# Order of the second batch's query pairs, and a fifth kind of pair by seven products

## The chip, the cores and the metric

The kernel runs on one core of a Trainium2 chip. A core has a matrix engine (TensorE, PE in the profile), a vector engine (VectorE, DVE), an activation engine (ScalarE, ACT), a general engine (GpSimd, POOL) and a queue that starts transfers (SyncE, SP). Each works through its own list of instructions in order; semaphores tie the lists together. Matrix products are written to PSUM[...]; everything else lies in SBUF. The metric is the device time of one execution in microseconds, as a median of several.

## The reference

The input x has 2 batches of 2048 rows of 512 numbers. It is normalised twice for an attention with one head of width 512 and a causal mask, and once for a mixture of experts whose output gates the attention's. All of it is computed in float32.

```python
xn = _layernorm(x)
# attention: a second norm, then
q, k, v = x_norm @ qkv[:, :512], x_norm @ qkv[:, 512:1024], x_norm @ qkv[:, 1024:]
scores = where(causal, q @ k.T / sqrt(512), -inf)      # per batch, 2048 x 2048
s = softmax(scores) @ v @ o_proj + xn
# experts: top 2 of 8, hidden width 352
g = silu(sum over the two experts of gate * expert(xn))
out = x + s * g
```

## The kernel before

The program first normalises all rows and makes keys, queries and values, which go to DRAM; then it runs the experts; the last part, from about 572 us on, is the attention, and only this part is touched by the change. The output projection has been folded into the values, so that attention ends with probabilities times values.

The attention works on tiles of 128 query rows. A batch has 16 tiles, 0 to 15, and 4 blocks of 512 keys. Tile t needs the key blocks before its own in full and its own block up to the diagonal, 128(t+1) keys in all. The list `seq` (line 1010) gives the tile of each of the 32 steps: the first batch in steps 0 to 15 from tile 15 down to tile 0, the second batch in steps 16 to 31 as line 1011 says. Two neighbouring tiles, an even one and the next, always follow each other: a pair. The blocks of the second batch are numbered 4 to 7, so K = 4 in the text below is the first of them.

In the loop at line 1756, step s does this for its tile:

- Scores. `chunk_scores` (line 1298) makes the scores of one key block, up to 512 wide, with four matrix products into a PSUM tile `ps`; a mask on the diagonal (line 1308) and a row maximum (line 1291) follow on VectorE. Pairs listed in `SCORED` (line 1267) go another way for their first two key blocks: `fast_scores` (line 1338) makes a 2 by 2 block product of the pair with seven half-size products (`p7`, line 1355) instead of eight, from sums of query parts (`query_sums`, line 1316, tile `sq`, made in the step before) and sums of key parts (`block_sums`, line 1327, tile `tk`, made once a batch). Each product is two calls 512 wide. The results are put together on VectorE (line 1361) in the tile `pT` in SBUF, both tiles of a pair at once in the pair's even step. ScalarE starts that with a copy of the first product (line 1374).
- `end_scores` (line 1389) negates the maximum; `exponentials` (line 1474) has ScalarE make the probabilities, piece by piece (line 1481).
- Turning. Probabilities must be transposed for the product with the values. Wide tiles go by GpSimd (line 1491, splitting the bytes), a transposing DMA (line 1497) and VectorE (`join_p`, line 1511). Tiles 0, 1 and 2 are transposed by TensorE one step later (`turn_p`, line 1504), with a copy by ScalarE (line 1509).
- Values, two steps later. `values` (line 1518) multiplies by one tile of 128 keys at a time, 512 wide, line 1531. Pairs in `FAST` (line 1268: those in `SCORED`, and pair 4 of the list) go by seven half-size chains instead (`values_first`, `values_next`, `values_end`, lines 1600 to 1651), from sums of probabilities (`combine_p`, line 1555) and sums of value parts (`combine_v`, line 1544, tile `vT`).
- Output. `divisor` sums and inverts (line 1653); `attended` scales on ScalarE (line 1692) and adds the residual on VectorE (line 1695); `emit` multiplies by the gate and adds x on GpSimd (lines 1703 and 1704) and stores. `gate` (line 1679) makes the gate of a pair: two scalings on ScalarE (line 1684), two sums on VectorE (line 1685), one Silu (line 1687). `gather_y` (line 1667) has GpSimd fetch the experts' rows.

The order of all this is written out by hand in the loop. Key and value blocks of the second batch are fetched while the first batch runs, by the list `parts_b` (line 1736): block 6 in steps 4 and 6, block 5 in steps 8 and 10, block 4 in steps 12 and 14, block 7 in steps 20 and 22. The table `later` (line 1742) says after which steps' exponentials the sums of key and value parts of the second batch are made, one part at a time. PSUM has two pools here: `ps_a` with five buffers for scores, `ps_b` with three for values; buffers are given in turn, so a product waits until the reader of the tile five places earlier is done.

Of the kernel before, what the change touches and what calls it, by code (L numbers as in the profile page):

```python
# [26 lines left out]
def gated_attention_moe(  # L27
# [33 lines left out]
    BT = 4  # L61
    TB = BT * P
    NB = NT // BT
    NBB = S // TB
# [943 lines left out]

    assert B == 2 and NBB == 4
    seq = [t for t in reversed(range(NBB * BT))]  # L1010
    seq += [NBB * BT + t for t in (8, 9, 0, 1, 6, 7, 2, 3, 4, 5, 10, 11, 12, 13, 14, 15)]
    assert all(seq[s] // 2 == seq[s + 1] // 2 for s in range(0, NT, 2))
    fetch_k = fetch(aks, lambda: kp2, kt_d, "k2", "kT")
    fetch_v = fetch(avs, lambda: vp, v_d, "v2", "v")
# [249 lines left out]
    OUT = 4  # L1264


    SCORED = (0, 1, 2, 3, 13, 14, 15)
    FAST = SCORED + (4,)

    def place(s):  # L1270
# [23 lines left out]
    def direct(s):  # L1294

        return range(2 if s // 2 in SCORED else 0, len(widths[s]))

# [18 lines left out]
    def query_sums(s, engine):  # L1316

        q = qsums[s] = sq.tile([P, 4, ND // 2, P], F32, name=f"sq_{s}", tag="sq")
        (a11, a12), (a21, a22) = (
            [aqs[seq[s] // 2][:, d, ts(seq[s + i] % 2, P)] for d in kds] for i in range(2)  # L1320
        )
        engine.tensor_tensor(q[:, 0], a21, a22, ALU.add)
        engine.tensor_tensor(q[:, 1], q[:, 0], a11, ALU.subtract)
        engine.tensor_tensor(q[:, 2], a11, a21, ALU.subtract)
        engine.tensor_tensor(q[:, 3], a12, q[:, 1], ALU.subtract)
# [341 lines left out]
    def gather_y(s):  # L1667

        rows[s] = [op.tile([P, 2, D], F32, name=f"yg0_{s}", tag="yg0")]
        for i in range(2):  # L1670
            rows[s].append(op.tile([P, D], F32, name=f"yg1_{s + i}", tag="yg1"))
            n = seq[s + i]
            for k, y in enumerate((rows[s][0][:, i, :], rows[s][-1])):
                nc.gpsimd.indirect_dma_start(  # L1674
                    out=y, out_offset=None, in_=y_d,
                    in_offset=bass.IndirectOffsetOnAxis(ap=posi[k][:, n : n + 1], axis=0),
                )
# [57 lines left out]
    K = NBB  # L1735
# [6 lines left out]
    later = {}  # L1742
    for steps, f, b in (
        ((10, 10, 11, 11), combine_v, K + 2), ((12, 12, 13, 13), combine_v, K + 1),
        ((20, 21, 22, 23), block_sums, K), ((24, 25, 26, 27), combine_v, K),
    ):
        for i, step in enumerate(steps):
            later.setdefault(step, []).append((f, b, (i + 1,)))
# [7 lines left out]
    for s in range(NT + OUT + 2):  # L1756
        fast = s // 2 - 1 in FAST
        pair = (s, s + 1) if s // 2 in SCORED else (s,)
        if s < NT and (s % 2 == 0 or len(pair) == 1):
# [30 lines left out]
        if s == NT - 1:  # L1790
            gather_y(NT - 2)
        if s % 2 and s > 3 and s // 2 + 1 in SCORED:
            query_sums(s + 1, nc.vector)
# [143 lines left out]
```

## Time and profile before

| what | us |
|---|---|
| median of 3 runs | 1010.59 |
| lowest and highest of them | 1010.33, 1010.79 |
| the profiled execution in all | 1012.02 |
| its span | 1010.3 |
| start of step 16 on TensorE (second batch) | 781.53 |
| start of the first pair by seven products in the second batch | 870.00 |
| end of TensorE's last product | 1006.48 |

The span runs from the first to the last instruction that the profile shows. All times below are microseconds from its start. A line of the timeline gives start, duration, engine, line of the program, operation, output and inputs without their numbers, and how often it came in a row; in brackets stands the idle time before it and who ended it. In the chain of waits each line is a stretch of the chain of work that ended last, with start, duration, engine, tile and line. A float32 matrix product appears as two records.

From 781.5 to 897.5 us, the steps that the change reorders, TensorE has no gap:

```profile
core 0: us, PE busy (x) PEld busy (x) DVE busy (x) ACT busy (x) POOL busy (x), PEclk, DMA share, GB/s
781.50:870.00 88.50, 88.50 (x247) 43.95 (x246) 54.35 (x98) 42.98 (x74) 66.45 (x55) 1.00 0.78 223
870.00:897.50 27.50, 27.50 (x68) 12.57 (x67) 22.58 (x44) 9.89 (x17) 15.15 (x13) 1.00 0.60 147
```

The columns are the stretch, its length, the busy time of each engine with the number of instructions, the clock that TensorE was granted, and the DMA engines' share and rate.

### The profile page before, as it was taken

To read this page: it belongs to the slowest core of one execution; us is meant where nothing else is said; L and a number is where in the kernel's file an instruction comes from. 1 tells how busy PE (TensorE), PEld (TensorE's weight loads), DVE (VectorE), ACT (ScalarE), POOL (GpSimd) and SP (SyncE) were. 2 spreads that over 40 slices of the span, in tenths; PEclk is the share of its full clock that TensorE was granted. 3 is DMA by queue.
4 is the path that set the end of the run, shared out by engine and by line. 5 is a ranking of instruction groups with operands and counts; after the bars stand their busy time and mean duration, and the time that the engine had idled before them with its cause. 6 is when DMAs were issued, how large, how long until landed. Compare 5 with 4: busy or idle time off the path is not lost. (4 is left out here: it accounts for less than half of the span.)

```text
span 1010.3 us, 13408 instructions
## 1 busy us (share of the span) xinstructions
PE 1001.5 (99%) x3924; PEld 665.7 (66%) x3924; DVE 719.6 (71%) x1396; ACT 402.7 (40%) x804; POOL 481.6 (48%) x475
## 2 busy tenths in 40 slices
PE   9999999999999999999999999999999999999998
PEld 5887888874577677667653448677675544447577
DVE  6997755896877777776744669678576457878667
ACT  3354455322444544444455122232345544442241
POOL 4474465003744444443432256164557776764272
PEclk9999999999999999999999999999999999999999
DMA  8799987979999999999999576373677768753361
GB/s 291 234 240 319 319 237 268 331 254 230 182 247 213 205 219 218 210 211 214 213 213 254 162 191 149 90 189 110 186 199 233 224 202 241 204 146 86 95 164 42
DMA packets 295495, 207.96 MB, mean 206 GB/s; under 512 B 230648, under 2 KB 243704, under 8 KB 294400
## 3 DMA queue, kind: packets, MB, share of 16 engines
q1 hardware_dynamic: 280128, 155.17, 62.1%
q0 software_dynamic: 10400, 34.63, 12.6%
q10 hardware_dynamic: 4896, 17.30, 4.6%
q8 instruction: 34, 0.56, 0.2%
q14 instruction: 37, 0.30, 0.1%
HBM read 92.35 MB, written 60.03 MB: 151 GB/s over the span
## 5 line engine op out<-in xcount | busy, mean ns | idle before, releaser
L1191 PE MATMUL py<-arena,ht 128*128 (+3 forms) x396 | 176.7, 593 | 0.0
L1303 PE MATMUL ps<-k,q 128*128 128x512 f32 (+3 forms) x416 | 143.0, 495 | 0.3 <-PEq L1451 0.3
L1491 POOL COPY pu<-pT 128x1024 uint16<-128x1024 uint16 (+2 forms) x74 | 81.8, 1137 | 119.1 <-ACT pT L1481 59.2
L1162 POOL COPY hu<-h 128x704 uint16<-128x704 uint16 x66 | 61.8, 954 | 155.8 <-issue 121.7
L1191 PEld LDWEIGHTS py<-arena,ht 128*128 128x128 f32 (+3 forms) x396 | 71.8, 185 | 80.6 <-issue 76.4
L1303 PEld LDWEIGHTS ps<-k,q 128*128 128x128 f32 x416 | 74.7, 190 | 67.1 <-issue 56.3
L966 POOL DMA_INDIRECT xs<-zu_d,toki x66 | 77.7, 1177 | 70.6 <-DVE toki L793 55.9
L1177 ACT ACTIVATE ht<-ht,b1sel 128x128 f32<-128x128 f32 (+3 forms) x216 | 67.9, 380 | 88.4 <-DVE ht L1171 88.4
L1141 DVE TENSOR_TENSOR h<-p,h 128x176 f32<-128x176 f32 x182 | 55.4, 336 | 59.6 <-PE p L1134 56.1
L1674 POOL DMA_INDIRECT yg<-y_d,posi x64 | 67.3, 1052 | 36.9 <-DVE yg L1685 22.0
L1531 PE MATMUL po<-v,pT 128*128 128x512 f32 x152 | 67.9, 592 | 0.0
L347 POOL COPY zu<-z 128x1024 uint16<-128x1024 uint16 x32 | 39.4, 1230 | 57.7 <-DVE z L332 57.7
L1481 ACT ACTIVATE pT<-pT,nm 128x1024 f32<-128x1024 f32 x14 | 16.1, 1148 | 110.3 <-DVE nm L1391 72.0
L1513 DVE COPY pT<-puT 128x1024 uint16<-128x1024 uint16 (+2 forms) x74 | 53.4, 750 | 7.4 <-DMA puT<-pu 7.2
L1199 ACT COPY y<-py 128x512 f32<-128x512 f32 x55 | 32.1, 584 | 62.1 <-PE py L1191 48.2
L1481 ACT ACTIVATE pT<-ps,nm 128x512 f32<-128x512 f32 (+3 forms) x52 | 30.0, 580 | 60.4 <-DVE nm L1391 36.7
L1361 DVE TENSOR_TENSOR pT<-p,pT 128x512 f32<-128x512 f32 x49 | 32.9, 687 | 25.8 <-PE p L1355 22.1
L1531 PEld LDWEIGHTS po<-v,pT 128*128 128x128 f32 x152 | 28.6, 190 | 31.9 <-issue 30.1
L1042 DVE COPY xT<-xhT 128x1024 uint16<-128x1024 uint16 x66 | 44.7, 703 | 6.4 <-DMA xhT<-xs 6.3
L1703 POOL TENSOR_TENSOR o<-o,yg 128x512 f32<-128x512 f32 x30 | 41.4, 1380 | 14.3 <-DVE o L1695 14.2
L1695 DVE SCALAR_TENSOR_TENSOR o<-xo,xscale,o 128x512 f32<-128x512 f32 x30 | 25.9, 871 | 30.1 <-ACT o L1692 30.1
L1704 POOL TENSOR_TENSOR o<-o,xo 128x512 f32<-128x512 f32 x30 | 43.2, 1439 | 2.4
(342 smaller groups left out, 2146.9 us busy)
## 6 DMA issues: line engine op xcount, KB each, us to landing
y_d<-y SPq DMA_DIRECT2D x66, 256.0 KB, 4.3
zu_d<-zu SPq DMA_DIRECT2D x32, 264.0 KB, 3.2
kt_d<-kT ACTq DMA_DIRECT2D x8, 1024.0 KB, 8.2
q<-qt_d SPq DMA_DIRECT2D x32, 256.0 KB, 5.0
k<-kt_d SPq DMA_DIRECT2D x32, 256.0 KB, 4.2
v<-v_d SPq DMA_DIRECT2D x32, 256.0 KB, 5.7
xo<-in_x_dram SPq DMA_DIRECT2D x32, 256.0 KB, 4.0
x<-in_x_dram SPq DMA_DIRECT2D x30, 256.0 KB, 6.5
```

What stands on the lines that cost most here:

```text
L966: nc.gpsimd.indirect_dma_start(out=xs, out_offset=None, in_=zu_d, in_offset=bass.IndirectOffsetOnAxis(ap=toki[:, order[i] : order[i] + 1], ...
L1042: nc.vector.tensor_copy(xT.bitcast(U16).rearrange("p c (t h) -> p c t h", h=2), xhs.pop(i).rearrange("p (h c) t -> p c t h", h=2),)
L1141: nc.vector.tensor_tensor(out, x, y, ALU.add)
L1162: nc.gpsimd.tensor_copy(hu[:, :, :H], h.bitcast(U16).rearrange("p (d h) -> p h d", h=2))
L1177: nc.scalar.activation(ht[:hn, c, at], ht[:hn, c, at], AF.Silu, bias=b1sel[:hn, c, j : j + 1])
L1191: nc.tensor.matmul(py[at, :], lhsT=ht[:k, c, at], rhs=rhs[n], start=(c == 0), stop=(c == NH - 1),)
L1303: nc.tensor.matmul(ps[:, :w], lhsT=aqs[seq[s] // 2][:, c, ts(t % 2, P)], rhs=aks[first + j][:, c, :w], start=(c == 0), stop=(c == ND - 1),)
L1481: nc.scalar.activation(turned[s][:, at:end], src, AF.Exp, bias=nm, accum_out=rs[:, j : j + 1])
L1491: nc.gpsimd.tensor_copy(pu[:, : 2 * w].rearrange("p (h d) -> p h d", h=2), turned[s][:, k : k + w].bitcast(U16).rearrange("p (d h) -> p h ...
L1513: nc.vector.tensor_copy(turned[s][:, k : k + w].bitcast(U16).rearrange("p (i t h) -> p i t h", t=P, h=2), puT[:, : 2 * w // P, :].rearrang ...
L1531: nc.tensor.matmul(dst, lhsT=turned[s][:, ts(k, P)], rhs=avs[first + k // BT][:, k % BT, cols], start=(start and k == k0), stop=(k == k1 - 1),
L1674: nc.gpsimd.indirect_dma_start(out=y, out_offset=None, in_=y_d, in_offset=bass.IndirectOffsetOnAxis(ap=posi[k][:, n : n + 1], axis=0),)
```

## The change

The pairs of the second batch come in another order, pair 8-9 moves from the front to the fifth place (steps 24 and 25) and is listed in `SCORED`, and so in `FAST`; it had been scored and multiplied in full. The value sums of block 4 move from steps 24 to 27 to steps 16 to 19, the key sums from steps 20 to 23 to steps 19 to 22. Pairs 10-11, 12-13 and 14-15 keep their steps, and the fetches keep theirs.

```diff
     seq = [t for t in reversed(range(NBB * BT))]
-    seq += [NBB * BT + t for t in (8, 9, 0, 1, 6, 7, 2, 3, 4, 5, 10, 11, 12, 13, 14, 15)]
+    seq += [NBB * BT + t for t in (6, 7, 4, 5, 0, 1, 2, 3, 8, 9, 10, 11, 12, 13, 14, 15)]
...
-    SCORED = (0, 1, 2, 3, 13, 14, 15)
+    SCORED = (0, 1, 2, 3, 12, 13, 14, 15)
     FAST = SCORED + (4,)
...
-        ((20, 21, 22, 23), block_sums, K), ((24, 25, 26, 27), combine_v, K),
+        ((16, 17, 18, 19), combine_v, K), ((19, 20, 21, 22), block_sums, K),
```

## Prediction

> **What bounds the kernel now.** I read the table of engines first, then the chain of waits in order of time, then VectorE's and ScalarE's timelines from 835 to 920 us, where the change acts.
>
> ```profile
> PE 1001.5 (99%) x3924; PEld 665.7 (66%) x3924; DVE 719.6 (71%) x1396; ACT 402.7 (40%) x804; POOL 481.6 (48%) x475
> ```
>
> TensorE works all the time; the others are partly idle. So time is saved by fewer TensorE instructions, and lost wherever TensorE has to wait. The chain shows both:
>
> ```profile
> 781.53 7.76 PE ps L1303 x24
> 789.29 1.72 PE po L1531 x4
> 791.01 0.11 PE pt L1508
> ...
> 870.00 12.02 PE p L1355 x28
> 882.02 2.58 PE ps L1303 x8
> 884.60 4.29 PE po L1531 x10
> ...
> 897.47 12.02 PE p L1355 x28
> ...
> 913.81 4.32 PE p L1579 x20
> ```
>
> Step 16, the first of the second batch, begins at 781.53, and from there each piece starts where the last one ended: no wait. A matmul call gives two records. A 512-wide call costs 12.02/14 = 0.859 us, a 256-wide one 4.32/10 = 0.432, and 128, 256 and 384 columns of scores (four calls) 0.89, 1.73 and 2.58. With these I can place every piece of a new order.
>
> The other engines are the danger:
>
> ```profile
> 845.64 2.37 DVE L1336 TENSOR_TENSOR tk<-k 128x1024 f32<-128x1024 f32 x1
> 847.93 1.75 DVE L1695 SCALAR_TENSOR_TENSOR o<-xo,xscale,o 128x512 f32<-128x512 f32 x1
> 865.58 1.25 DVE L1322 TENSOR_TENSOR sq<-q 128x256 f32<-128x256 f32 x1
> 866.86 0.50 DVE L1323 TENSOR_TENSOR sq<-sq,q 128x256 f32<-128x256 f32 x1
> 867.29 1.48 DVE L1324 TENSOR_TENSOR sq<-q 128x256 f32<-128x256 f32 x1
> 868.69 1.48 DVE L1325 TENSOR_TENSOR sq<-q,sq 128x256 f32<-128x256 f32 x1
> ...
> 877.67 3.41 DVE L1361 TENSOR_TENSOR pT<-p,pT 128x512 f32<-128x512 f32 x5 [1.69 <-ACT pT L1374]
> ```
>
> ```profile
> 872.34 0.69 ACT L1481 ACTIVATE pT<-ps,nm 128x512 f32<-128x512 f32 x1 [7.79 <-DVE nm L1391]
> ...
> 876.11 1.06 ACT L1687 ACTIVATE yg<-yg 128x1024 f32<-128x1024 f32 x1
> 877.07 0.57 ACT L1374 COPY pT<-p 128x512 f32<-128x512 f32 x1
> ```
>
> A pair by seven products starts at 870.00, but its first VectorE add runs at 877.67: it waits for ScalarE's copy of the first product (877.07), which is queued behind the last step's exponential (872.34) and the gate's Silu. That exponential waits for VectorE (7.79 us).
>
> [...]the same 128x256 subtraction takes 0.41 and 1.48 us, and the long ones lie beside GpSimd copies and sums. [...]
>
> **The change, part by part.**
>
> *Products.* Tiles 8 and 9 take keys of 512+512+128 and 512+512+256. Scores of the two full blocks: 2x2x4 = 16 calls become 14, saving 1.72 us. Values: 9+10 = 19 calls of 0.859 (16.31) become seven chains of 4 half-wide calls plus 6 half-wide calls for the remaining key tiles, 34 x 0.432 = 14.69, saving 1.62. Together 3.34 us of TensorE, the only gain. Reordering removes no products, and pairs from 10-11 on stand as before.
>
> *Sums moved.* V sums (four of about 0.7 us) go from steps 24-27 to 16-19, block sums (1.20 to 2.37) from 20-23 to 19-22. The first V sum waits for the V block whose loads are issued at 782.35 to 784.9 and take 5.7 us: landed by 790.6, when VectorE gets there (step 16's scores end at 787.5, plus about 2.8 of maxima and reciprocal). Behind it is only the output sum that in the old trace waited for ScalarE until 795.23. I cost it at nothing; bound 0 to 0.5.
>
> *Added on VectorE for pair 8-9:* four query sums in step 23, seven adds of 0.69, one 1024-wide maximum more, four sums of probabilities (0.7), seven adds of 0.42: about 17 us, less some narrower maxima, where TensorE has 3.3 us less to cover them. GpSimd's copies stay; SyncE issues the same loads and transposes in another order. The query of pair 8-9 follows output stores that wait for GpSimd: free at 826.4, issued near 830.5, plus 6.7 to land: 837-838, before its use at 840.5.
>
> *The new order on TensorE, without waits, from 781.53:* step 16 ends 789.4, 17 at 797.1, 18 at 807.4, 19 at 819.5. Step 20: scores 820.4, values 824.7. Step 21: 826.4, 831.5, transpose 831.6. Step 22: 834.2, 835.1, 835.3. Step 23: 838.7, 840.5, 840.8. Seven products of step 24: 852.8, then 853.7, 856.3; step 25: 858.0, 861.4; seven of step 26 from 861.4. Steps 22 and 23 are short (3.7 and 5.5 us), because tiles 0-3 now follow each other.
>
> *Who is late.* ScalarE after the transpose at 831.5, by the pitches of 819.65 to 824.66 in the old trace: copy 831.7, exponential 831.8, gate scaling 832.3, Silu 834.9, output 835.9, copy 836.7, table 837.0, exponential of step 22 at 838.4 (used at 840.5: 1.5 us spare), next output 838.9 to 839.7. VectorE: output sum 836.7, mask and maximum to 838.2, reciprocal; at 838.5 the last block sum. GpSimd multiplies and adds outputs until about 843, so I take means: block sum 1.82 (840.3), output sum 0.93 (841.2), four query sums (4.52+4.12+3.42)/3 = 4.0 (845.2), mask, maximum and negation 1.15: exponential of step 23 at 846.4. Without contention (1.20, 0.67, 1.45) it is 843.0; with all of it (2.37, 1.67, 4.5), 848.2.
>
> *From there to TensorE.* Exponential to first add takes 4.9 us (872.34 to 877.67 less one 256-wide exponential): 851.3, so the seventh product, which needs the copy of the first, waits 0.2. From the first add of a pair to the next step's exponential the old trace has 19.74 us (877.67 to 897.41); less 1.2, for which the output copy waited for TensorE, and 0.8 of wider pieces, 17.7 remain: 869.0 for the exponential of step 25, its second part done at 870.6. By the built program's waits the fifth product of step 26 takes the PSUM buffer that this exponential reads. It is due at 868.5, so TensorE, which works in order, loses 2.1 there with all that stands behind. The copy for the seventh product ends 6.2 after the exponential (897.41 to 903.72), at 875.2, against 874.0: 1.2 lost. The first sum of probabilities of pair 8-9 is ready 9.7 after the first add (904.32 to 916.24, less 0.7 of waiting, 0.8 of a blocked output sum and 0.7 of wider pieces): 884.9 against 883.4, 1.5 lost. The add that frees the half bank for the pair's last chain follows 12.2 later (916.24 to 930.89, less 1.4 of waiting and about 1 for shorter sums): 897.1 against 896.5, 0.6 lost. Together 0.2+2.1+1.2+1.5+0.6 = 5.6 us. The old order has slack in the same places, as two pairs by seven begin 27.5 us apart there (870.00, 897.47); now the first two begin 20.6 apart.
>
> *Sum.* -3.3 + 5.6 = +2.3 us on a span of 1010.3 (the profiled execution took 1012.02 in all, the median of the runs is 1010.59; I add the difference to the median): 1012.9. Every microsecond by which the exponential of step 23 moves, moves the sum by about one: 843.0 gives stalls of some 2 and a net of -1.3; 848.2 gives +4.1.
>
> **Rivals.**
> - *All hidden, the other side:* VectorE reaches the exponential of step 23 before 842, so that step 26's products find their buffers free: -3.3, 1007.3. For it: VectorE is busy 71%, block and V sums leave the steps of pair 8-9, and my 17.7 and 12.2 us are pieced together from a busier stage. Against: 843.0 is already the uncontended sum. It decides at about 844.0: earlier is a gain, later a loss.
> - *Half hidden:* contention is mild and stalls are 2 to 5 us: 1009.3 to 1012.3, no change. For it: of the four block sums two took 1.2 to 1.5 and two 2.2 to 2.4, so contention comes and goes.
> - *More than that:* the query of pair 8-9 lands late. If GpSimd's store of step 17's output slips by 3 us, step 24 itself stalls, and all after it: 1016. Against: 2.5 us spare by my sum.
> - That the new products aren't made is excluded: the new instruction order has all 14 score calls and 34 half-wide value calls.
>
> **How the numbers follow.** Late chain (stalls of 5 to 7.5 us; own range 1011.5 to 1014.8) 0.41, half hidden 0.20, all hidden 0.33, late query 0.06. About 0.2% (2.0 us) is what a measurement of this kernel can tell from no change: below 1008.6 is faster, above 1012.6 slower. Late chain gives 0.33 slower and 0.08 same, half hidden 0.16 same and 0.04 faster, all hidden 0.32 faster and 0.01 same, late query 0.06 slower: 0.36 faster, 0.25 same, 0.39 slower. Predicted is the likeliest, 1012.9; the range 1007.2 to 1015.0 takes in the other side.
>
> **What would show it.** Right: TensorE idle before the fifth or seventh product of step 26 and before the first chain on probability sums of pair 8-9, released by the exponential, the copy and the VectorE sums; step 28's seven products start after 897.5. Wrong: these start at 894.2 with no wait in the chain, or the waits lie elsewhere (steps 18 to 22, a query load, the first V sum).

## The result, and the profile after

The changed kernel takes 1016.69 us (median of 6 runs, 1015.55 to 1018.39); the kernel before took 1010.63 beside it (6 runs, 1010.33 to 1011.09). The ratio is 1.0056, interval 1.0046 to 1.0066: slower by 6.06 us. The forecast was slower by 2.3 (1012.9, range up to 1015.0). Of all the executions below one was in a slow state (of gate_behind, 1165.48 us at a mean clock of 0.85); it counts in that run's median, which is 1012.28 without it, but not in its ratio.

The profiled execution of the changed kernel took 1016.27 us, its span is 1014.6. In its chain of waits step 16 starts at 779.79 and the last product ends at 1010.75:

```profile
779.79 6.02 PE ps L1303 x16
...
1008.98 1.74 PE p L1531 x8
1010.75 0.50 DVE o L1723
```

That start is 1.74 us sooner than in the profile of before, and the part ahead of it is the same in both programs; so I compare the stretch from the start of step 16 to the end of the last product. It was 224.95 us (781.53 to 1006.48) and is 230.96: 6.01 more, close to what the medians say. (The timeline puts the start of step 16 0.16 us ahead of the chain's in both profiles, so all four times are taken from the chain.) The table of engines of the changed kernel:

```profile
PE 1000.6 (99%) x3950; PEld 672.3 (66%) x3950; DVE 735.2 (72%) x1417; ACT 403.0 (40%) x802; POOL 483.6 (48%) x475
```

Against the line of before, TensorE's busy time went down by 0.9 us only, although 3.3 us of products are gone: part of the rest ran at a lower clock (1.75 us more, below). VectorE got 15.6 us more. TensorE, which had no gap in this stretch before, now waits five times. The timeline of TensorE, the lines with a wait (start, duration, engine, line, operation, tiles, shapes, count, and the idle time with its releaser):

```profile
839.84 3.67 PE L1355 MATMUL p<-k,q 128*128 128x512 f32 x8 [0.81 <-DVE tk L1336]
844.34 5.42 PE L1355 MATMUL p<-tk,sq 128*128 128x512 f32 x12 [0.84 <-DVE sq L1323]
...
870.34 1.99 PE L1355 MATMUL p<-tk,sq 128*128 128x512 f32 x4 [1.65 <-ACT pT L1481]
...
875.09 1.99 PE L1355 MATMUL p<-tk,q 128*128 128x512 f32 x4 [1.04 <-ACT pT L1374]
...
885.57 3.53 PE L1579 MATMUL p<-vT,s 128*128 128x256 f32 x8 [2.03 <-DVE s L1573]
```

These are, in order: the first product of step 24, its third product, the fifth and the seventh of step 26, and the first chain on sums of probabilities of pair 8-9. Placed by the durations of the pieces, each start is late by a little more than its bracket says: 0.97, 1.07, 1.81, 1.31 and 2.30 us (the fifth product, say, was due at 861.66 + 4 x 1.717 = 868.53). Together 7.46; about 0.1 more is lost behind the third product of step 24. The first line's releaser is a key sum that the product doesn't read. What it does read is the query of pair 8-9, whose two loads were issued at 833.18, behind a store that waited for GpSimd until 832.25 and behind four key loads of block 7, issued from 829.23 on.

The remaining loss isn't a wait. The table by stretches (stretch, length, busy time of PE, PEld, DVE, ACT, POOL, then the clock that TensorE was granted, DMA share and GB/s):

```profile
core 0: us, PE busy (x) PEld busy (x) DVE busy (x) ACT busy (x) POOL busy (x), PEclk, DMA share, GB/s
882.00:884.00 2.00, 1.54 (x8) 1.01 (x6) 1.97 (x5) 0.00 (x0) 0.00 (x0) 1.00 0.93 313
884.00:886.00 2.00, 0.43 (x2) 0.40 (x3) 1.97 (x5) 1.15 (x2) 0.00 (x0) 0.95 0.27 101
886.00:888.00 2.00, 2.00 (x6) 1.59 (x5) 1.97 (x3) 0.92 (x5) 1.84 (x2) 0.50 0.00 0
888.00:890.00 2.00, 2.00 (x8) 1.67 (x7) 1.97 (x6) 0.00 (x0) 2.00 (x3) 0.70 0.61 116
890.00:892.00 2.00, 2.00 (x8) 1.25 (x7) 1.97 (x3) 0.00 (x0) 1.92 (x2) 1.00 0.92 178
```

Right after the longest wait (2.03 us) the clock falls to half: in slices of half a microsecond it was 0.80 from 885.5, 0.50 from 886.0 to 889.0 and 0.78 up to 889.5. The eight half-wide calls that follow the wait take 1.75 us more than at full clock, 5.21 (885.57 to 890.78) in place of 8 x 0.432. The ledger is then 7.46 + 0.1 + 1.75 = 9.3 us of loss against 3.3 of saved products, net 6.0.

Why the waits are there is seen on VectorE and ScalarE. VectorE's timeline in steps 22 and 23 (the lines between the last key sum and the negated maximum of step 23):

```profile
837.17 2.64 DVE L1336 TENSOR_TENSOR tk<-k,tk 128x1024 f32<-128x1024 f32 x1
839.73 1.75 DVE L1695 SCALAR_TENSOR_TENSOR o<-xo,xscale,o 128x512 f32<-128x512 f32 x1
841.40 1.48 DVE L1322 TENSOR_TENSOR sq<-q 128x256 f32<-128x256 f32 x1
842.92 1.37 DVE L1323 TENSOR_TENSOR sq<-sq,q 128x256 f32<-128x256 f32 x1
844.21 0.41 DVE L1324 TENSOR_TENSOR sq<-q 128x256 f32<-128x256 f32 x1
844.55 0.41 DVE L1325 TENSOR_TENSOR sq<-q,sq 128x256 f32<-128x256 f32 x1
...
845.93 0.15 DVE L1391 TENSOR_REDUCE nm<-mx 128x1 f32<-128x1 f32 x1
```

There is no idle time between these lines: the key sum, the output sum, four query sums, mask and maximum come one after the other. GpSimd multiplies and adds outputs from 837.43 to 844.01, and as soon as it stops, a sum of 128x256 takes 0.41 us in place of 1.37 to 1.48. (The second query sum, begun at 842.92, ends at 844.29, just behind GpSimd's instruction.) ScalarE's timeline from there on:

```profile
846.12 0.69 ACT L1481 ACTIVATE pT<-ps,nm 128x512 f32<-128x512 f32 x1 [6.52 <-DVE nm L1391]
...
850.39 0.57 ACT L1374 COPY pT<-p 128x512 f32<-128x512 f32 x1
...
868.60 1.15 ACT L1481 ACTIVATE pT<-pT,nm 128x1024 f32<-128x1024 f32 x1 [7.47 <-DVE nm L1391]
869.74 0.45 ACT L1481 ACTIVATE pT<-ps,nm 128x256 f32<-128x256 f32 x1
...
873.51 1.06 ACT L1687 ACTIVATE yg<-yg 128x1024 f32<-128x1024 f32 x1 [0.69 <-DVE yg L1685]
874.47 0.57 ACT L1374 COPY pT<-p 128x512 f32<-128x512 f32 x1
```

The exponential of step 23 starts 6.28 us after step 24's first product. 22.48 us later comes the exponential of step 25, whose end frees the PSUM buffer of the fifth product of step 26; 5.87 later the copy that the seventh product waits for. Between exponential and copy ScalarE makes a gate, 4.3 us: two scalings, a load of the table for Silu (1.28 us), and a Silu that waits for VectorE.

### The profile page after: what moved, and what is told of

Same layout as the page of the kernel before. It is cut to its first block, busy times and chain, and to the rows that moved or that the text cites. A ratio compares the mean times of both kernels' runs of the same rounds, so it can differ in the third digit from the quotient of the medians.

```text
span 1014.6 us, 13477 instructions
## 1 busy us (share of the span) xinstructions
PE 1000.6 (99%) x3950; PEld 672.3 (66%) x3950; DVE 735.2 (72%) x1417; ACT 403.0 (40%) x802; POOL 483.6 (48%) x475
## 5 line engine op out<-in xcount | busy, mean ns | idle before, releaser
L1491 POOL COPY pu<-pT 128x1024 uint16<-128x1024 uint16 (+3 forms) x74 | 81.8, 1137 | 128.0 <-issue 66.7
L1303 PE MATMUL ps<-k,q 128*128 128x512 f32 (+3 forms) x384 | 129.2, 487 | 0.3 <-PEq L1451 0.3
L1303 PEld LDWEIGHTS ps<-k,q 128*128 128x128 f32 x384 | 68.8, 191 | 59.4 <-issue 48.5
L1481 ACT ACTIVATE pT<-pT,nm 128x1024 f32<-128x1024 f32 x16 | 18.4, 1149 | 130.7 <-DVE nm L1391 89.4
L1361 DVE TENSOR_TENSOR pT<-p,pT 128x512 f32<-128x512 f32 x56 | 37.7, 687 | 30.6 <-PE p L1355 26.8
L1513 DVE COPY pT<-puT 128x1024 uint16<-128x1024 uint16 (+3 forms) x74 | 52.0, 733 | 9.5 <-DMA puT<-pu 9.2
L1531 PE MATMUL po<-v,pT 128*128 128x512 f32 x114 | 51.2, 593 | 0.0
L1481 ACT ACTIVATE pT<-ps,nm 128x512 f32<-128x512 f32 (+3 forms) x48 | 27.3, 571 | 56.0 <-DVE ri L1655 29.3
L1579 PE MATMUL p<-vT,s 128*128 128x256 f32 x180 | 43.4, 390 | 2.0 <-DVE s L1573 2.0
L1355 PE MATMUL p<-tk,sq 128*128 128x512 f32 x96 | 42.9, 595 | 2.5 <-ACT pT L1481 1.7
```

The source lines that it names most:

```text
L1303: nc.tensor.matmul(ps[:, :w], lhsT=aqs[seq[s] // 2][:, c, ts(t % 2, P)], rhs=aks[first + j][:, c, :w], start=(c == 0), stop=(c == ND - 1),)
L1355: nc.tensor.matmul(ps, lhsT=x[:, c], rhs=y[:, c], start=(c == 0), stop=(c == ND // 2 - 1))
L1491: nc.gpsimd.tensor_copy(pu[:, : 2 * w].rearrange("p (h d) -> p h d", h=2), turned[s][:, k : k + w].bitcast(U16).rearrange("p (d h) -> p h ...
L1513: nc.vector.tensor_copy(turned[s][:, k : k + w].bitcast(U16).rearrange("p (i t h) -> p i t h", t=P, h=2), puT[:, : 2 * w // P, :].rearrang ...
L1531: nc.tensor.matmul(dst, lhsT=turned[s][:, ts(k, P)], rhs=avs[first + k // BT][:, k % BT, cols], start=(start and k == k0), stop=(k == k1 - 1),
L1579: nc.tensor.matmul(dst, lhsT=a[:, k], rhs=v(k), start=(k == 0), stop=(stop and k == n - 1))
```

## The experiments

Each batch of runs had runs of the kernel before beside it; their medians were 1010.68 to 1011.11. "Ratio" is to those, with its 95% interval; it rests on all executions, so it isn't always the quotient of the two medians. The changed kernel's own is 1.0056 [1.0046, 1.0066].

| run | us | ratio |
|---|---|---|
| order_only | 1017.01 | 1.0063 [1.0048, 1.0077] |
| sums_back | 1020.02 | 1.0082 [1.0068, 1.0097] |
| mid_before | 1016.63 | 1.0057 [1.0045, 1.0069] |
| wide_before | 1017.70 | 1.0069 [1.0056, 1.0082] |
| key_sums_early | 1018.40 | 1.0082 [1.0065, 1.0098] |
| both_early | 1019.30 | 1.0085 [1.0071, 1.0099] |
| alt_67 | 1019.72 | 1.0091 [1.0075, 1.0106] |
| alt_45 | 1018.31 | 1.0086 [1.0072, 1.0100] |
| gate_behind | 1012.62 | 1.0013 [1.0005, 1.0022] |
| gate_behind_45 | 1015.60 | 1.0047 [1.0033, 1.0060] |
| gate_behind_old | 1011.24 | 1.0002 [0.9994, 1.0010] |
| gate_behind_q | 1011.45 | 1.0008 [0.9997, 1.0019] |
| sums_18_21 | 1015.32 | 1.0055 [1.0038, 1.0072] |
| loads_24 | 1017.19 | 1.0061 [1.0047, 1.0074] |
| order_loads_24 | 1012.49 | 1.0011 [0.9999, 1.0023] |
| all_sooner | 1011.24 | 1.0004 [0.9995, 1.0012] |
| all_sooner_2 | 1013.62 | 1.0022 [1.0015, 1.0030] |
| sums_only | 1010.76 | 0.9996 [0.9987, 1.0005] |

The theories that the expectations name: the first four runs set a "chain theory" (the late chain of the prediction) against the order as such. From then on A is that chain: VectorE reaches the exponential of step 23 late, and from there a sequence of fixed length over the gate and the copy sets the waits in steps 26 and 27. B says that the late query and the short steps (first batch of runs with it), or simply too much work on VectorE (later ones), sets them whatever the chain; C that two pairs by seven products are too close together in any order; D that a key sum is in the way wherever it stands; E that the loads of block 7 crowd the other transfers.

### The parts of the change alone: order_only, sums_back, sums_only

order_only keeps order and sums and scores pair 8-9 in full again:

```diff
-    SCORED = (0, 1, 2, 3, 12, 13, 14, 15)
+    SCORED = (0, 1, 2, 3, 13, 14, 15)
```

> The new order and the earlier sums, but pair 8-9 scored and multiplied in full (SCORED as before). Chain theory (the pair by seven in steps 24 and 25 comes too close behind short steps and too close before the next pair by seven): its cause is gone and TensorE's products are those of the kernel before, so 1009.5 to 1012, no wait of TensorE in steps 23 to 27. Rival, order (tiles 0 to 3 in a row are what costs): still some 5 us slower than before, 1014 to 1017. Rival, moved sums: also slower than before, 1013 or more.

Measured 1017.01: as slow as the whole change. This was a miss for my first theory, in which the seven products' chain was the whole loss. The new order costs some 6 us without them, and that comes about in another way. VectorE's timeline of order_only in step 24:

```profile
849.76 0.68 DVE L1291 TENSOR_REDUCE mx<-ps 128x1 f32<-128x512 f32 x1
857.76 0.69 DVE L1513 COPY pT<-puT 128x1024 uint16<-128x1024 uint16 x1 [7.32 <-DMA puT<-pu]
858.37 0.68 DVE L1291 TENSOR_REDUCE mx<-ps 128x1 f32<-128x512 f32 x1
```

and TensorE's lines with waits just behind it:

```profile
860.64 1.99 PE L1303 MATMUL ps<-k,q 128*128 128x256 f32 x8 [2.17 <-ACT pT L1481]
...
871.10 5.42 PE L1355 MATMUL p<-tk,sq 128*128 128x512 f32 x12 [1.59 <-ACT pT L1481]
```

VectorE sits idle for 7.32 us at a join, since the transposed tile of step 23 hasn't landed, and the other two maxima of step 24 stand behind the join. Without them there is no exponential, and without it no free PSUM buffer for the scores of step 25. (A wait of 0.98 us at the start of step 24 comes before these, as in the change.) I first read this as a price of the order as such; order_loads_24 below shows what it was.

sums_back takes the other part back: the sums of keys and values at their old steps, the rest as changed.

```diff
-        ((16, 17, 18, 19), combine_v, K), ((19, 20, 21, 22), block_sums, K),
+        ((20, 21, 22, 23), block_sums, K), ((24, 25, 26, 27), combine_v, K),
```

> The changed kernel with the sums of block 4 at their old steps (key sums 20 to 23, value sums 24 to 27). Chain theory: the value sums add four times 0.7 us to the chain that is late, and the third of them is needed by TensorE in step 26: slower than the changed kernel by 1 to 4 us, 1017.5 to 1021. Rival, moved sums: faster than the changed kernel, towards 1012 or below.

Measured 1020.02, as the chain theory said. The sum of value parts now stands in TensorE's way itself (2.92 us at 891.37, released by VectorE, tile `vT`, line 1553). So in the new order the moved sums are a help.

sums_only is the opposite, the old order and products with the sums where the change puts them:

> The kernel before with the key and value sums of block 4 in the changed kernel's steps; order and products as before. All theories: TensorE has slack there, no change, 1010.3 to 1011.5. If the moved sums had a cost of their own it would show here.

Measured 1010.76, no difference, and no wait of TensorE in the trace. With this each part has run alone or been taken out: the order costs, the sums cost nothing in the old order and help in the new one, and the seven products, added to the new order, neither gain nor lose (order_only and the change have the same time). The seven products in the old order were not run.

### Other orders: mid_before, wide_before, alt_67, alt_45

Four orders, each with pair 8-9 fifth and by seven products:

```diff
-    seq += [NBB * BT + t for t in (6, 7, 4, 5, 0, 1, 2, 3, 8, 9, 10, 11, 12, 13, 14, 15)]
+    seq += [NBB * BT + t for t in (6, 7, 2, 3, 0, 1, 4, 5, 8, 9, 10, 11, 12, 13, 14, 15)]
...
+    seq += [NBB * BT + t for t in (4, 5, 2, 3, 0, 1, 6, 7, 8, 9, 10, 11, 12, 13, 14, 15)]
...
+    seq += [NBB * BT + t for t in (6, 7, 0, 1, 4, 5, 2, 3, 8, 9, 10, 11, 12, 13, 14, 15)]
...
+    seq += [NBB * BT + t for t in (4, 5, 0, 1, 6, 7, 2, 3, 8, 9, 10, 11, 12, 13, 14, 15)]
```

> Order 6-7, 2-3, 0-1, 4-5, 8-9 with the seven products kept: steps 22 and 23 get 3.1 us more of TensorE work and the two first pairs by seven begin 24.1 instead of 20.6 us apart. Chain theory: waits of TensorE in steps 23 to 27 fall from 9.5 to 1 to 3 us, so 1008 to 1010.5. Rival, VectorE work (a fifth pair by seven has more VectorE work than can be covered in any place): 1012 to 1016, waits of 5 us or more. Rival, order of small tiles: 1008 to 1016, no statement.

> Order 4-5, 2-3, 0-1, 6-7, 8-9 with the seven products kept: steps 22 and 23 get 6.5 us more of TensorE work and the two first pairs by seven begin 27.5 us apart, as two of the kernel before. Chain theory: no waits of TensorE in steps 23 to 27, at most 1.5 us in step 18, where the first tile's probabilities have less cover: 1007 to 1009. Rival, VectorE work: 1012 or more.

> The change with the order 6-7, 0-1, 4-5, 2-3, 8-9 in place of 6-7, 4-5, 0-1, 2-3, 8-9: small and wide pairs alternate, so that steps 22 and 23 have 6.9 and 8.6 us of TensorE's work in place of 3.7 and 5.5; products are the same. Theory A (the backlog comes from four short steps in a row just ahead of pair 8-9): the exponential of step 23 comes about 2 us after the start of step 24, few or no waits: 1007.3 to 1009.5. Theory C (two pairs by seven products 20.6 us apart are too close whatever comes before): waits of 2 to 6 us in steps 26 and 27 stay, 1010 to 1014.

> The change with the order 4-5, 0-1, 6-7, 2-3, 8-9: steps 22 and 23 have 8.6 and 10.3 us of TensorE's work. Theory A: 1007.3 to 1009.5 as in alt_67, unless the steps 16 to 18, shorter here, make a query late (1.3 us of waiting was seen at step 18 when pair 4-5 stood first): then up to 1011. Theory C: 1010 to 1014.

In all four the chain theory (A in the last two) missed, with 1016.63, 1017.70, 1019.72 and 1018.31; only for wide_before does a rival's range, "1012 or more", hold the result. A longer step just ahead of pair 8-9 moves the waits to other places and doesn't remove them. Where they went, by the lines with waits: in mid_before to a value product of step 21 (2.37 us, a divisor's sum on VectorE) and the fourth product of step 24 (2.93); in wide_before to a query load (1.32), a join (2.51), a value product with no releaser named (0.89), a divisor's sum (2.72) and the fourth product of step 24 (1.19); in alt_67 to three joins (1.31, 1.32, 0.75) and 1.70 us with no releaser named, with the waits of step 26 still behind them; in alt_45 to a query load (1.91) and 1.94 us ahead of a value product for which the profile names no releaser.

alt_45 still tells something about the chain, since its step 24 begins without a wait (847.26). Its exponential of step 23 comes at 847.89, 0.63 us after that, and TensorE's only wait from there to step 28 is

```profile
888.65 1.97 PE L1579 MATMUL p<-vT,s 128*128 128x256 f32 x8 [2.02 <-DVE s L1573]
```

With the chain started on time, the waits before the fifth and seventh product of step 26 are gone. The wait for the sums of probabilities is there all the same: it comes from the copy of step 26 and what follows it, not from how late the chain began.

### Taking away what makes VectorE late: key_sums_early, both_early, sums_18_21, loads_24

```diff
key_sums_early, both_early
-        ((16, 17, 18, 19), combine_v, K), ((19, 20, 21, 22), block_sums, K),
+        ((16, 17, 18, 19), combine_v, K), ((16, 17, 18, 19), block_sums, K),
both_early
-        if s % 2 == 0 and NQ <= n < NT // 2:
+        if s % 2 == 0 and NQ <= n < NT // 2 and s != 22:
...
+        if s == 21:
+            for c in range(2):
+                fetch_q(12, c)
sums_18_21
-        ((16, 17, 18, 19), combine_v, K), ((19, 20, 21, 22), block_sums, K),
+        ((16, 17, 18, 19), combine_v, K), ((18, 19, 20, 21), block_sums, K),
loads_24
-               (12, fetch_k, K), (14, fetch_v, K), (20, fetch_k, K + 3), (22, fetch_v, K + 3)]
+               (12, fetch_k, K), (14, fetch_v, K), (24, fetch_k, K + 3), (26, fetch_v, K + 3)]
```

> The change with the four key sums of block 4 in steps 16 to 19 in place of 19 to 22. Theory A (VectorE's backlog before the exponential of step 23 sets every later wait): the last key sum (2.64 us, 837.17 to 839.81 in the changed kernel) is gone from step 22, the exponential of step 23 comes at 843.6 to 844.8 in place of 846.12, and the waits in step 26 shrink by as much: 1013.5 to 1015.5 us. Theory B (the late query of pair 8-9 and the shortness of the steps 20 to 23 set it): no change, 1016 to 1017.5.

Measured 1018.40, slower than the change. The trace shows why, and that the late waits didn't change. TensorE's lines with waits in key_sums_early:

```profile
826.58 7.08 PE L1531 MATMUL po<-v,pT 128*128 128x512 f32 x12 [2.29 <-DVE pT L1513]
872.46 1.98 PE L1355 MATMUL p<-tk,sq 128*128 128x512 f32 x4 [1.65 <-ACT pT L1481]
877.21 1.98 PE L1355 MATMUL p<-tk,q 128*128 128x512 f32 x4 [1.05 <-ACT pT L1374]
887.69 2.90 PE L1579 MATMUL p<-vT,s 128*128 128x256 f32 x8 [2.03 <-DVE s L1573]
```

The join of a transposed tile became late in step 21 (2.29 us, with half clock after it: 0.78, 0.50 and 0.87 in the slices of 2 us from 826 to 832): VectorE, with eight sums in steps 16 to 19, came to it at 825.51 in place of 823.10. The two waits at the start of step 24 are gone, and the three in steps 26 and 27 stand as in the changed kernel, to 0.01 us.

> As key_sums_early, and the query of pair 8-9 is fetched in step 21, ahead of the store of step 17's output on SyncE. Theory A: the query lands at about 837, before its use at 838.9, but the exponential of step 23 comes when it did in key_sums_early, since the query sums wait behind other work on VectorE, so TensorE waits elsewhere for the same chain: within 0.5 us of key_sums_early. Theory B (the late query is a loss of its own): 0.8 to 1.2 us below key_sums_early.

The edit put the fetch behind step 21's scores, which is still behind the store on SyncE, so the query wasn't really early and the run doesn't answer its question. It took 1019.30, with the same three waits (1.64, 1.04, 2.01).

> The change with the key sums of block 4 one step sooner, steps 18 to 21 in place of 19 to 22. Theory A (the exponential of step 23 starts a chain of fixed length): without the last key sum (2.64 us) VectorE starts step 23's work when ScalarE's output copy is done, so the query sums and the exponential of step 23 come 1.6 us sooner; the wait before the third product (1.07) goes, those in step 26 shrink by about 1: 1013.5 to 1015.7. Theory D (every key sum is in the way of something wherever it stands, as in key_sums_early): a join of a transposed tile is late in step 21 and gives it back: 1016 to 1018.

Median 1015.32, inside theory A's range, but the interval of the ratio (1.0038 to 1.0072) holds the changed kernel's too, so the time alone decides nothing. In the trace both theories have a part: the third product of step 24 no longer waits, a join in step 21 does (0.80 us), and step 26 waits 1.85, 1.05 and, before the chain on sums, 2.04.

> The change with the loads of block 7 in steps 24 and 26 in place of 20 and 22. Theory A: the query of pair 8-9 lands in time and its wait (0.96) goes, but the third product then waits longer for the query sums, which stand behind other work on VectorE; nothing is gained: 1016 to 1017.3. Theory E (the loads crowd the queries and the transposes, and that is the loss): 1013.5 to 1015.5.

Measured 1017.19, theory A. The query is in time (step 24 starts at 838.98 without a wait), and the third product waits longer, for the query sums on VectorE:

```profile
844.63 7.11 PE L1355 MATMUL p<-tk,sq 128*128 128x512 f32 x12 [2.06 <-DVE sq L1323]
```

Counted from the start of step 16 the exponentials of steps 23 and 25 come within 0.2 us of where they came in the change. (Half clock follows the wait here, 0.74, 0.50 and 0.91 in the slices of 2 us from 844 to 850, which is new, and the fifth product then comes too late to wait.) So the late query, which I had given a rival of its own, costs nothing: it lies beside the longer queue of VectorE. With the key loads of block 7 no longer ahead of them the query's loads landed in time; so those were part of what made it late.

### The chain itself: gate_behind and its relatives

gate_behind makes the gate that stood between exponential and copy after the copy instead, in steps 24 and 26. The output that uses it moves along.

```diff
+    GATE_BEHIND_COPY = (24, 26)
...
         add(c21, made(q[:, 2], k[:, 2]), c12)
+        if s in GATE_BEHIND_COPY:
+            gate(s - 4)
+            emit(s - 4)
         p5 = made(q[:, 0], k[:, 0])
...
-            if s == (k + 2 if k + 2 in AHEAD else k + 3):
+            if s == (k + 2 if k + 2 in AHEAD else k + 3) and s + 1 not in GATE_BEHIND_COPY:
                 gate(k)
```

> The change, with the gate of pair 4 places back (its two scalings and the Silu on ScalarE, its two sums on VectorE, and the output that needs it) made in steps 24 and 26 behind ScalarE's copy of the first product, in place of ahead of it at the end of steps 23 and 25. Theory A (a fixed chain sets the waits: exponential of step 23, gate, copy, seven adds, exponential of step 25, gate, copy, sums of probabilities): the copies come 3 to 4 us sooner after the exponential, the waits before the fifth and seventh product of step 26 and before the first chain on sums (1.81, 1.32, 2.30 us) go, and the lower clock after them (1.92) with them; those at the start of step 24 (0.96, 1.07) stay: 1009 to 1011. Theory B (VectorE has too much work in steps 24 to 27, whatever starts it): part of the waits stay, 1013 to 1016.

Measured 1012.62: 4 us off the change, and the only edit of one thing that took off this much. ScalarE's timeline in gate_behind (its lines are numbered one to four higher):

```profile
871.97 1.15 ACT L1485 ACTIVATE pT<-pT,nm 128x1024 f32<-128x1024 f32 x1 [7.47 <-DVE nm L1395]
...
873.57 0.57 ACT L1375 COPY pT<-p 128x512 f32<-128x512 f32 x1
...
877.54 1.06 ACT L1691 ACTIVATE yg<-yg 128x1024 f32<-128x1024 f32 x1 [0.87 <-DVE yg L1689]
```

The copy comes 1.60 us after the exponential in place of 5.87. TensorE's two last lines with a wait are

```profile
847.95 7.11 PE L1356 MATMUL p<-tk,sq 128*128 128x512 f32 x12 [2.01 <-DVE sq L1324]
...
885.86 1.97 PE L1583 MATMUL p<-vT,s 128*128 128x256 f32 x8 [0.25 <-DVE s L1577]
```

The wait before the seventh product is gone, and of the 2.03 before the chain on sums 0.25 is left, with no half clock after it (1.00 from 854 to 912). The wait before the fifth is gone in this profile too, but not by the gate: TensorE came to it later. What is left is a join in step 21 (0.67 us) and a longer wait of the third product of step 24 (2.01, for the query sums) with half clock behind it (0.74, 0.50 and 0.91 in the slices of 2 us from 848 to 854). Theory A left 2 us for the start of step 24, about what is lost there, but nothing for the join and for a half clock; its range ends at 1011, and even the fastest execution took 1011.09. The profiled execution is the slowest of the twelve normal ones (1014.86), but its step 16 also starts late: from there to the last product it takes 3.7 us less than the change's profile. Both lose 1.7 us of clock between 780 and 912, and the mean clock of both executions was 0.998, so the gain isn't one of the clock.

With other runs in which pair 8-9 goes by seven products the chain can be laid out (us, from the traces):

| run | exponential of step 23 after the start of step 24 | to the exponential of step 25 | to the copy of step 26 |
|---|---|---|---|
| the change | 6.28 | 22.48 | 5.87 |
| key_sums_early | 5.49 | 22.48 | 5.87 |
| alt_67 | 4.28 | 22.46 | 5.88 |
| sums_18_21 | 6.22 | 22.48 | 5.87 |
| loads_24 | 7.43 | 22.48 | 5.87 |
| alt_45 | 0.63 | 23.80 | 5.87 |
| gate_behind | 7.38 | 22.25 | 1.60 |
| gate_behind_q | 6.52 | 21.19 | 1.60 |
| gate_behind_45 | 0.63 | 25.03 | 1.59 |

The third column depends only on where the gate stands. The second is 22.5 us in each of these runs with the gate in its old place and a late start, and between 21.2 and 25.0 in the others. TensorE needs 27.5 us from the start of step 24 to the fifth product of step 26 (20.64 + 6.87, the pieces of alt_45) and the exponential of step 25 runs for 1.7 us. So with 22.5 us in the second column the fifth product is free of a wait only if the first is below 3.3 (alt_67, with 4.28, waits 0.82). In the changed kernel it was 6.28, 2.9 too much; about 1.2 of that TensorE had already lost at the third product of step 24, which leaves about 1.8 to wait, as in the trace (1.81). So what is lost at the third product of step 24 and before the fifth of step 26 is one lateness in two parts: less in one place is more in the other. The move of the gate shortens the third column.

> gate_behind with the order 4-5, 0-1, 6-7, 2-3, 8-9. In alt_45 the waits before step 24 were 1.91, 1.94 and 0.17 us and a lower clock, behind it only the one before the first chain on sums, 2.02. Theory A: that one goes, the others stay: 1015 to 1017. Theory B: it stays, 1018 to 1019.

1015.60, as theory A said: alt_45's late wait fell from 2.02 to 0.25, its early ones stayed (1.68 for a query, 2.37 before a value product).

> The kernel before with the gate of step 26 behind the copy of the first product; a control. TensorE has no wait there, so both theories expect no change: 1010.3 to 1011.3. A larger difference would be an effect of the moved gate itself.

1011.24, no change, as expected: in the old order, where TensorE has no wait to lose, the place of the gate is of no account.

gate_behind_q adds to gate_behind the key sums in steps 18 to 21 and a fetch of the query that really stands ahead of the store (`stores` holds the outputs that would have been stored in step 21):

```diff
-        ((16, 17, 18, 19), combine_v, K), ((19, 20, 21, 22), block_sums, K),
+        ((16, 17, 18, 19), combine_v, K), ((18, 19, 20, 21), block_sums, K),
...
+        if s == 21:
+            for c in range(2):
+                fetch_q(12, c)
+            for k in stores:
+                emit(k)
```

> gate_behind with the key sums of block 4 one step sooner (steps 18 to 21) and the query of pair 8-9 fetched in step 21, ahead of the store of step 17's output. Theory A: the exponential of step 23 and the query sums come about 2.6 us sooner, the waits at the start of step 24 go as well: 1007.3 to 1008.8. If the sooner key sums make a join of a transposed tile late, as in key_sums_early (2.3 us and a lower clock): 1010 to 1013.

1011.45, in the second range: TensorE waits 1.04 us for a join in step 21, still 1.14 at the third product of step 24, 0.37 at the fifth of step 26 and 0.27 at the first chain on sums. The interval (0.9997 to 1.0019) overlaps that of gate_behind.

### Why the order alone is slow: order_loads_24

order_only with the loads of block 7 (the edit of loads_24):

> order_only (the change without the seven products of pair 8-9) with the loads of block 7 in steps 24 and 26. In order_only VectorE sat idle for 7.32 us until the transposed tile of step 23 landed, with the maxima of step 24 behind it. Theory E (the transposing transfer was behind the loads of block 7): it lands some 6 us sooner, the waits of 2.17 and 1.59 us go: 1012 to 1014. Theory A: the transfer is late for another reason, 1016 to 1017.5.

Measured 1012.49, in theory E's range: 4.5 us of order_only's 6 go when eight loads start four steps later. The same join on VectorE, and the wait of TensorE that is left behind it:

```profile
855.04 0.83 DVE L1513 COPY pT<-puT 128x1024 uint16<-128x1024 uint16 x1 [3.20 <-DMA puT<-pu]
...
868.50 5.42 PE L1355 MATMUL p<-tk,sq 128*128 128x512 f32 x12 [1.25 <-ACT pT L1481]
```

The wait of 2.17 us and the 0.98 at the start of step 24 are gone; the 1.59 is 1.25, and a join in step 21 is new (1.21). So theory E said too much of the second wait. This is the profile of a slower execution (1014.22; the 13 lie between 1010.77 and 1015.74).

From the issue of the transposing transfer to the join it was 11.6 us in order_only (846.12 to 857.76), with the four value loads of block 7 issued at 842.99, right ahead of it; here it is 7.5 (847.52 to 855.04). In the changed kernel the same move of the loads does nothing (loads_24): VectorE has adds of the seven products to make before it comes to that join (856.83, with no idle time before it), so the late tile is covered.

### In search of a version that beats both: all_sooner, all_sooner_2

all_sooner is gate_behind_q with the loads of loads_24, and the query sums of step 24 at the end of step 22. all_sooner_2 further has

```diff
-        ((16, 17, 18, 19), combine_v, K), ((18, 19, 20, 21), block_sums, K),
+        ((16, 17, 18, 19), combine_v, K), ((17, 18, 20, 21), block_sums, K),
...
-            if s == 22:
-                query_sums(24, nc.vector)
+            if s in (22, 25):
+                query_sums(s // 2 * 2 + 2, nc.vector)
```

with the query sums of step 26 no longer ahead of the maxima of step 25.

> gate_behind_q with the loads of block 7 in steps 24 and 26 and the query sums of step 24 at the end of step 22, where VectorE was idle for 1.15 us. Theory A: the exponential of step 23 comes 1 to 2 us sooner and the third product doesn't wait; what stays is a join of about 1 us in step 21: 1008 to 1010, below the kernel before. Theory B (VectorE has too much work whatever the order): 1011 to 1012.5.

> all_sooner with the query sums of step 26 behind the exponential of step 25 in place of ahead of its maxima, and the first two key sums in steps 17 and 18 in place of 18 and 19. Theory A: the exponential of step 25 comes about 3.7 us sooner, the waits before the fifth product of step 26 (1.20) and before the first chain on sums (0.27) go, the third product waits 0 to 0.5, the join in step 21 is in time or nearly: 1008.5 to 1010.3, below the kernel before. Theory B (VectorE's work comes out somewhere else): 1010.5 to 1012.

Neither did. all_sooner took 1011.24, level with the kernel before (0.9995 to 1.0012) and above its range of 1008 to 1010. all_sooner_2 took 1013.62, worse, and above the ranges of both theories. TensorE waits 1.43 us in step 21 there (826.87, no releaser named) and in step 26, where the lines are, of VectorE

```profile
864.55 2.33 DVE L1517 COPY pT<-puT 128x1024 uint16<-128x1024 uint16 x3 [1.19 <-DMA puT<-pu]
...
867.57 0.42 DVE L1324 TENSOR_TENSOR sq<-sq,q 128x256 f32<-128x256 f32 x1
```

and of TensorE

```profile
868.05 5.42 PE L1356 MATMUL p<-tk,sq 128*128 128x512 f32 x12 [2.39 <-DVE sq L1324]
```

With the query sums out of the way VectorE comes to the joins before their tiles have landed, waits 1.19 us, and makes the query sums after that, too late for the third product of step 26. This is what theory B said, though not how much: in each arrangement that I ran with the seven products something on VectorE is late between steps 21 and 27. Whether another one could bring out the 3.3 us stays open.

## Why the prediction was right or wrong

**The gain: right.** TensorE's pieces have the predicted lengths; 3.3 us of products are gone.

**Steps 16 to 22: right.** TensorE has no wait there, and sums_only shows that the moved sums are free in the old order.

**The mechanism and the places: right from step 26 on.** The fifth and seventh product of step 26 and the first chain on sums wait, for the exponential, the copy and VectorE's sums as said. The lost times there were predicted as 2.1, 1.2 and 1.5 and are 1.81, 1.31 and 2.30. The half of a PSUM buffer for the last chain (0.6) was free in time. In step 24 the places were wrong: the sum had 0.2 before the seventh product, which didn't wait, and nothing for the query (0.97) and for the third product, which needs the second query sum (1.07). A wait for a query load was among the prediction's own signs of being wrong.

**The links of the chain: right but for one.** Exponential to first add was taken as 4.9 and is 4.87 (846.12 to 850.99); first add to the exponential of step 25 as 17.7, is 17.61; first add of step 26 to the first sum as 9.7, is 10.35 (875.07 to 885.42). gate_behind shows that the gate in this chain is a cause, and one that can be taken out. The prediction saw the copy queued behind the Silu, but took it as given.

**The start of the chain: wrong, the first failing step.** The sentence "so I take means: block sum 1.82 (840.3), output sum 0.93 (841.2), four query sums ... = 4.0 ...: exponential of step 23 at 846.4" averaged over free and contended instances. On the prediction's axis (1.74 us later) the exponential came at 847.9, 1.5 late: the key sum began 0.4 late and took 2.64, the output sum took 1.75. GpSimd was at its outputs through these two and the first two query sums, as the prediction itself said in the same sentence ("until about 843"; it was until about 845.8), so the contended figure was the one to take for them. The last two query sums were free, and the four took 3.5 us, less than the mean. (No run moves GpSimd's outputs away; the contention is read from these durations alone.) The prediction's own rule for full contention ("848.2 gives +4.1") would have given 1014.7, still 2.0 short.

**The query: a loss that isn't one.** It came 0.97 us late, the rival with a chance of 0.06; the predicted 2.5 us of slack was eaten by a store that waited for GpSimd, with the loads of block 7 in the way as well. Its loads were issued at 833.18 in place of about 828.8 (830.5 less 1.74). That this rival's 1016 is nearer to the measured time than the forecast is chance: the claim that "all after it" would move with it was wrong, as loads_24 takes this wait away and gains nothing.

**The clock: put at nothing, the second failing step.** The sum places every piece at full clock; 1.75 us were lost after the wait that ended at 885.57, at half clock (0.50 from 886.0 to 889.0). Together: 2.3 predicted, 1.5 by the start of the chain, 0.7 by the link to the first sum, 1.8 by the clock, less 0.6 for the last chain makes 5.7 of 6.0.

**What the prediction didn't ask.** The prediction took the order as free but for the pair that moved. order_only shows that this order costs as much with the full products, 4.5 us of it through loads (order_loads_24) that it only counted as "the same loads and transposes in another order". That order_only and the change take the same time is then no sign of one cause.

## What to carry to other kernels

Where two engines contend over a stretch, lay their timelines over each other and take the contended or the free duration for each instruction (1.37 to 1.48 or 0.41 us for a sum of 128x256 here); a mean of both is right for neither. Before making a stage shorter, look at the chain on the other engines from one of its instances to the next, and at what stands in their queues only by habit: a gate, a sum or a load that was hidden for as long as the stage was long. Moving one such item in front of another was no gain here, where VectorE's queue was full (key_sums_early, loads_24); what took 4 us and more off was a removal from the chain (gate_behind) or from the transfers ahead of it (order_loads_24).

## What the hardware showed

TensorE's clock fell to half in or right after waits of only 1.9 to 2.9 us (1.91 in alt_45, 2.93 in mid_before), in some executions and not in others. In the profile of the changed kernel the shares at 884 to 890 add up to 1.7 us of lost clock (0.05 x 2 + 0.50 x 2 + 0.30 x 2). Summed like this from 780 to 912, nine of 18 profiles (all but those of all_sooner_2 and sums_only) lose clock, and each loses 1.7 (this one and gate_behind) or 3.4 us (sums_back, mid_before, key_sums_early, both_early, alt_45, loads_24, gate_behind_45). The 22 executions of all_sooner_2 fall into two groups by their mean clock: ten at 1.0 with a median of 1012.39 us, twelve at 0.998 with 1014.13; the distance of 1.74 us is about one such loss of 1.7. So a wait of 2 us can cost nearly twice its length, 2.03 + 1.75 = 3.78 in the changed kernel. It need not: shorter waits (1.65 here and 1.85 in sums_18_21, each before a fifth product) had a clock of 1.00 behind them, and one of 2.72 in wide_before had too. Why the clock falls after one wait and not after another of the same length, these runs don't show.
